# Attention and gated FFN on one core: the second product of the output projection earlier, and VectorE's multiplications of P @ v ahead of the joining step and the subtraction

## The chip, the core and the metric

The kernel runs on one core of a Trainium2 chip. The metric is the device time of one execution in microseconds (us); the median of several executions counts. Engines: TensorE (PE in the profile, its weight loads PEld), VectorE (DVE), ScalarE (ACT), GpSimd (POOL), and SyncE (SP), which issues the transfers here. Each engine has its own list of instructions.

## The reference

Input is 8 sequences of 256 tokens with 512 features, all float32. One attention layer and one FFN layer, each behind a layer norm and with a residual:

```
x = x + attention(layernorm(x))         # 32 query heads, 8 key/value heads, D = 128
x = x + ffn(layernorm(x))

attention: q, k, v = x @ w_qkv
           scores = q k^T / sqrt(128) - slope[head] * sqrt(distance), causal
           out = softmax(scores) @ v, then @ w_o
ffn:       dense = x @ weight.T + bias
           hits = softmax(x @ centroids.T / 0.1) > 0.01
           out  = dense where the row has a hit and the column's cluster has one, else 0
```

## The kernel before

**Units and slots.** The eight sequences form four pairs p of 512 tokens. For each pair and each key/value head kv there is a group g = 8 p + kv, and each group has two units, one for each sequence of the pair: u = 2 g + bb. A unit is the attention of four query heads over one sequence. The main loop (line 660) runs over the units; one turn of it is called a slot here, and `slot = u % 16` (line 663) says where in the pair it stands. Even slots have bb = 0, odd ones bb = 1. A slot takes about 22 us and holds three units at different stages:

- of unit u: the scores on TensorE (L376 and L382), scaled and biased by VectorE (L378, L384), and the maxima of the softmax;
- of unit u − 1: the subtraction of the maxima, two thirds by GpSimd (L428) and one third by VectorE (L431), the exponential by ScalarE (L754), and its sums;
- of unit u − 2: the product P @ v on TensorE (L452, L453; `attend`), VectorE's multiplication by the inverse sums (L456, two of them, one for each two heads, which write oT), and the output projection (`project_out`, whose matmuls are L474).

Keys lie on the partitions, so a maximum or sum over keys goes over partitions. `over_keys` does it in three VectorE steps: two reductions with a 32x32 transpose (L393 over the first 128 keys, L394 over the others) and the joining step (L396), which combines the two. `over_quadrants` (called from `rows` and `rows_max`) does the rest: TensorE transposes the small tile r (L403, tile tp_r), VectorE reduces it to a row, and SyncE writes the row to HBM and reads it back broadcast to all partitions (tile bc). The next slot's subtraction and multiplication use bc.

**Seven products.** All projections are done by a scheme with seven matrix products instead of eight (as Strassen's). Sums of the operand's blocks are named S1 to S4 for one side and T1 to T4 for the other; S3 is written over block A21. A step function takes the number of a product: steps 1, 6, 7, 4 go one after the other into one PSUM bank and are copied out by ScalarE after each; a copy must be done before the next of them starts. Step 2 goes into a bank of its own and VectorE adds it; steps 5 and 3 share a bank, and VectorE adds after each. The factors: step 1 takes A11 and B11, step 2 A12 and B21, step 5 S1 and T1, step 6 S2 and T2, step 7 S3 and T3, step 3 S4 and B22, step 4 A22 and T4. Three such projections run interleaved in a slot:

- `qq(i)`: the q projection of the next group (tiles ps_qa, ps_qb, ps_qc), spread over the even slot (1, 2, 6, 7) and the odd one (4, 5, 3);
- `e(i)`: in slots 0, 1, 8, 9 the v projection (ps_va, ps_vb, ps_vc), in slots 3, 7, 11, 15 the k projection (ps_ka, ...), in the others nothing;
- `w(i)`: the output projection of unit u − 2 (ps_oa, ps_ob, ps_oc). Its sums S1 to S4, tile o_s, are made by GpSimd out of oT (lines 112 to 118, called at line 783). A11 and A12 are parts of oT itself.

For the v projection the sums S3 and S4 of the weights are made by VectorE in slots 0 and 8 (line 746, tile wv and e_t). In slots 11 and 12 the normed tokens of the next pair are transposed (`x(i)`, tile tpx, copied out by ScalarE, one PSUM bank). Pairs 1 and 2 carry the FFN of the pair before in slots 3 to 6 (`f(part)`). `norm(part)` computes layer norms; its square root and the exponential need different tables of ScalarE, so a table load stands before the first exponential after a norm.

**Order.** There is no scheduler: `tc.manual_schedule()` keeps every engine's instructions in the order of the program text. That order is the list of calls at lines 798 to 820, one for even slots, one for odd ones, and others for the first and last slots. An instruction waits for its inputs and for its buffers, and everything behind it on its engine waits with it. `max_and_old` (line 740) issues the third scores, the maxima of unit u (L393, L394, L396), the subtraction L431 for unit u − 1, and in slots 0 and 8 S3 and S4. `exp_old` issues L754.

Of the kernel before, what the change touches and what calls it, by code (L numbers as in the profile page):

```python
# [17 lines left out]
ALU = mybir.AluOpType  # L18
AX = mybir.AxisListType
# [4 lines left out]
G = NH // NKV  # L24
# [29 lines left out]
def block_kernel(  # L54
# [12 lines left out]
    nc = tc.nc  # L67
# [21 lines left out]
    gp, ve = nc.gpsimd.tensor_tensor, nc.vector.tensor_tensor  # L89
# [17 lines left out]
    def a_sums(tt, a, which="S1 S2 S3 S4"):  # L107
        for s in which.split():
            if callable(a[s]):
                a[s] = a[s]()  # L110
            if s == "S1":
                tt(a["S1"], a["A21"], a["A22"], ALU.add)  # L112
            elif s == "S2":
                tt(a["S2"], a["S1"], a["A11"], sub)
            elif s == "S3":
                tt(a["S3"], a["A11"], a["A21"], sub)
            else:
                tt(a["S4"], a["A12"], a["S2"], sub)
# [64 lines left out]
    wv, wk, wq, wo = {}, {}, {}, {}  # L183
# [176 lines left out]
    K0, K1 = G * S, G * P  # L360
    J0, J1 = K0 // 32, K1 // 32
    s_sb, inv_sb, bc_sb = {}, {}, {}
# [24 lines left out]

    def over_keys(s, r, which, op):  # L390
        a, b = which * J0, 2 * J0 + which * J1
        first, second = r[:, a : a + J0], r[:, b : b + J1]
        nc.vector.tensor_reduce(first, s[:, :K0].rearrange("p (j q) -> p j q", q=32), AX.X, op, apply_transpose=True)  # L393
        nc.vector.tensor_reduce(second, s[:, K0:].rearrange("p (j q) -> p j q", q=32), AX.X, op, apply_transpose=True)  # L394
        late = first.rearrange("p (h i) -> p h i", h=G)[:, :, 4:8]
        nc.vector.tensor_tensor(late, late, second.rearrange("p (h i) -> p h i", h=G), op)  # L396

    def over_quadrants(u, r, has_max, has_sum):

# [24 lines left out]
    def subtract_max(u, i):  # L424
        s, mx = s_sb[u], bc_sb[u][:, 0]
        if i == 0:
            k0 = s[:, :K0].rearrange("p (h q) -> p h q", h=G)
            gp(k0, k0, mx, sub)  # L428
        else:
            k1 = s[:, K0:].rearrange("p (h q) -> p h q", h=G)  # L430
            ve(k1, k1, mx[:, :, P:], sub)  # L431
# [209 lines left out]
    k, q = project_k(0, 0), project_q(0)  # L641
# [18 lines left out]
    for u in range(NU + 2):  # L660
        g, bb = divmod(u, 2)
        p, kv = divmod(g, NKV)
        slot = u % SPP
        own, old, out_ = u < NU, 0 < u <= NU, u >= 2
        more_q, more_p = own and g + 1 < NG, own and p + 1 < NPAIR
        r = small.tile([P, 2 * (J0 + J1)], F32, tag="r", name="r", bufs=2) if own or old else None
# [13 lines left out]
        e, qq = nothing, nothing  # L680
        if own and u > 0 and slot in (0, 1, 8, 9):
            e = project_v(p, slot // 8, bb)
        elif own and slot in (3, 7, 11):
            e = project_k(p, (slot + 1) // 4)
        elif more_p and slot == 15:
            e = project_k(p + 1, 0)
        if more_q:
            if bb == 0:
                q = project_q(g + 1)
            qq = q  # L690
        ww = {}

        def w(*steps):
            for i in steps:
                if out_:
                    if i == 1:
                        ww[0] = project_out(u - 2)
                    ww[0](i)


        t_ffn = None
        if own and 3 <= slot < 7 and 0 < p < NPAIR - 1:
            t_ffn = (p - 1) * TPP + slot - 3
# [3 lines left out]
        def f(part):  # L707
            if t_ffn is not None:
                if part == 0:
                    ffn_transpose(t_ffn)  # L710
                elif part == 1:
                    ffn_second(t_ffn, w_ffn)
                elif part == 1.5:
                    ffn_first(t_ffn, w_ffn)
                    ffn_max(t_ffn)
                    ffn_exp(t_ffn)
                elif part == 2:
                    ffn_bias_add(t_ffn, y_late[:, t_ffn % TPP, :] if t_ffn >= first_late else None)
                else:
                    ffn_hits(t_ffn)  # L720
                    ffn_qsel(t_ffn)
                    ffn_end(t_ffn)
# [12 lines left out]
        def norm(part):  # L735
            nonlocal found
            if t_norm is not None:
                found = (lambda _: norm_stats(t_norm, t_norm + 1), norm_root, norm_scale, norm_write)[part](found)

        def max_and_old():  # L740
            scores(u, 2)
            over_keys(s_sb[u], r, 0, ALU.max)
            if u > 1:
                subtract_max(u - 1, 1)
            if u > 0 and slot in (0, 8):
                a_sums(ve, wv[p, slot // 8], "S3 S4")

        def more_sums():
            if more_p and slot == 14:
                sum_x(p + 1, "T3 T4")  # L750

        def exp_old():
            if u > 1:
                nc.scalar.activation(s_sb[u - 1], s_sb[u - 1], AF.Exp)  # L754

        def sum_old():
            if old:
                over_keys(s_sb[u - 1], r, 1, ALU.add)
# [3 lines left out]
        def rows_max():  # L762
            if alone:
                over_quadrants(u, r, True, False)

        def rows():
            if old:
                over_quadrants(u, r, own and not alone, True)

        def behind_rows():  # L770

            f(3)
            norm(2)
            if own and (slot == 7 or slot == 15 and more_p):
                sum_weights(ve, wv, (p, 1) if slot == 7 else (p + 1, 0), HH, "S1 S2")
            if more_p and slot == 13:
                sum_x(p + 1, "T1 T2")

        def av(i):
            if out_:  # L780
                attend(u - 2, i)
                if i == 1:
                    a_sums(gp, o_sb[u - 2][1])

        def x(i):
            if more_p and slot in (11, 12):
                norm_tile(p + 1, 2 * (slot - 11) + i)

        if u == 0:
            k(3), max_and_old()  # L790
            sum_weights(ve, wv, (0, 0), HH, "")
            e = project_v(0, 0, 0)
            q_first("5p"), e(1), e(2), q_first(5), q_first(3), rows_max()
            a_sums(ve, wv[0, 0])
            qq(1), e(6), qq(2), e(7), e(5), qq(6), e(4), e(3), qq(7)
            subtract_max(0, 0), subtract_max(0, 1)
            nc.scalar.activation(s_sb[0], s_sb[0], AF.Exp)
        elif bb == 0 and own:
            qq(1), e(1), max_and_old(), e(2), f(0), av(0), e(6), exp_old(), av(1), more_sums(), f(1), rows_max(), f(1.5), e(7), qq(2)
            if u == 4:  # L800
                onehot_of_columns(asg)
            f(2), norm(0), e(5), e(4), qq(6), e(3), x(0), w(1), x(1), sum_old(), w(5, 6), norm(1), qq(7), w(2)
            rows(), behind_rows(), w(7, 3), norm(3), w(4)
        elif u < NU - 1:
            e(1), qq(4), e(2), max_and_old(), f(0), e(6), av(0), exp_old(), e(7), av(1), f(1), f(1.5), e(5), qq(5)
            f(2), norm(0), e(4), e(3), x(0), w(1), x(1), sum_old(), w(5, 6), norm(1), qq(3), w(2)
            rows(), behind_rows()
            if u == NU - 3:
                found_late = norm_scale(norm_root(found_late))
            w(7, 3), norm(3), w(4)  # L810
        elif own:

            max_and_old(), f(0), av(0), exp_old(), av(1), rows_max(), f(1), f(1.5)
            f(2), w(1), sum_old(), w(5, 6), w(2)
            rows(), subtract_max(u, 0), subtract_max(u, 1)
            w(7)
            norm_write(found_late)
            nc.scalar.activation(s_sb[u], s_sb[u], AF.Exp)
            w(3), w(4)
            t_old = t_ffn  # L820
        elif bb == 0:
            sum_old(), av(0), f(0), av(1), f(1), rows()
            ffn_first(t_ffn, w_ffn), w(1, 5)
            ffn_max(t_ffn), ffn_exp(t_ffn)
            f(2), w(6)
            flush_adds()
            ffn_hits(t_old), ffn_qsel(t_old), ffn_end(t_old)
            w(2, 7)
            flush_adds()
            w(3, 4)  # L830
            found = norm_stats(last, last + 1)
            t_old = t_ffn
        else:
            av(0), f(0)
            found = norm_scale(norm_root(found))
            av(1), norm_write(found, tags=("y", "y")), f(1)
            ffn_hits(t_old), ffn_qsel(t_old), ffn_end(t_old)
            ffn_max(t_ffn), ffn_exp(t_ffn)
            w(1, 2, 5, 6, 3)
            found = norm_root(norm_stats(last + 2))  # L840
            w(7)
            ffn_transpose(last, "bc")
            ffn_transpose(last + 1, "snap", tp=p_long.tile([P, 512], F32, tag="aq", name="tpx_late"))
            norm_write(norm_scale(found))
            w(4)
            normalise(norm_stats(last + 3))
            ffn_first(t_ffn, w_ffn)
# [144 lines left out]
```

## Time and profile before

| what | value |
|---|---|
| median of 3 runs | 1426.2 us (1426.0 to 1427.32) |
| profiled execution, its time | 1425.68 us |
| profiled execution, its span | 1423.9 us |
| TensorE clock granted | 0.999 |
| busy: VectorE, GpSimd, ScalarE | 933.7, 878.9, 370.9 us |
| the chain that ended last: PE, DVE, issue, POOL | 91%, 6%, 1%, 1% |
| exponential L754 (128x1536) | 62 times, mean 1484 ns |
| GpSimd's subtraction L428 (128x1024) | 64 times, mean 2372 ns |
| joining step L396 (128x16) | 128 times, min 174, median 272, max 2101 ns |

The span runs from the first instruction to the last in one profiled execution; the execution's time has 1.8 us around it. In the lists of waits, a line gives the engine, the tile and line that waited, after the arrow who released it, then the total, the number and the longest of these waits in us. In a timeline, a line gives the start, the length, the engine, the line of the kernel, the operation, output and inputs with their shapes, and in brackets how long the engine had idled before and who ended that. A line "x4" merges four records; a float32 matmul leaves two records.

### The profile page before, as it was taken

Reading aid. Unit: us, or ns where it says so; the run is one execution under the profiler, and the core shown is the slowest. Engines: PE = TensorE matmul, PEld = TensorE weight load, DVE = VectorE, ACT = ScalarE, POOL = GpSimd, SP = SyncE. Lnnn points to the kernel's source line nnn. Section 1 sums busy time; section 2 is a strip of 40 time slices with the busy share of each in tenths; the row PEclk is TensorE's granted clock in tenths of the full one; section 3 lists DMA queues with packets and bytes.
Section 4 is the critical chain, followed back from the end, with each engine's and each line's share of the span. In section 5 each row is a group of like instructions: output and inputs, shape, how many; then the busy total and the mean of one; then the engine's idle time right before and its main releaser. Section 6 shows DMA issues by size and latency. Waiting matters only on the chain.

```text
span 1423.9 us, 16581 instructions
## 1 busy us (share of the span) xinstructions
PE 1402.3 (98%) x5867; PEld 1082.6 (76%) x5867; DVE 933.7 (66%) x1723; ACT 370.9 (26%) x649; POOL 878.9 (62%) x878
## 2 busy tenths in 40 slices
PE   9999999999999999999999999999999999999997
PEld 7777777767878777777777777777787778777674
DVE  5557666686566665668656667566766566556878
ACT  2222223411232222341223222243222122212332
POOL 5587857767465654668656466565756666476663
PEclk9999999999999999999999999999999999999999
DMA  5335343443242544423334435344314342333343
GB/s 188 119 106 175 123 125 132 144 148 128 96 167 75 178 141 157 157 81 142 126 113 143 132 120 178 126 156 149 133 60 148 130 168 88 148 102 125 133 163 118
DMA packets 87312, 190.20 MB, mean 134 GB/s; under 512 B 11616, under 2 KB 20064, under 8 KB 87232
## 3 DMA queue, kind: packets, MB, share of 16 engines
q1 hardware_dynamic: 86320, 187.59, 38.5%
q10 hardware_dynamic: 864, 1.44, 0.3%
q8 instruction: 47, 0.77, 0.2%
q14 instruction: 33, 0.27, 0.1%
q0 software_dynamic: 48, 0.13, 0.0%
HBM read 176.03 MB, written 13.11 MB: 133 GB/s over the span
## 4 chain that ended last, share of the span: by engine, by line
PE 91%; DVE 6%; issue 1%; POOL 1%; ACT 0%; DMA 0%; DVEq 0%; POOLq 0%; ACTq 0%
PE ps_oa L474 15%; PE ps_qa L145 14%; PE ps_oc L474 8%; PE sc L376 7%; PE ps_qc L145 7%; PE av L452 7%; PE ps_ka L145 4%; PE sc L382 4%; PE ps_va L145 4%; PE ps_ob L474 4%; PE av L453 3%; PE ps_qb L145 3%; PE ps_vc L145 2%; PE ps_kc L145 2%; PE ps_lg L520 2%; PE ps_f L520 1%
## 5 line engine op out<-in xcount | busy, mean ns | idle before, releaser
L428 POOL TENSOR_TENSOR s<-s,bc 128x1024 f32<-128x1024 f32 x64 | 151.8, 2372 | 157.3 <-DMA bc<-row_hbm 157.2
L506 POOL TENSOR_TENSOR x<-x,snap 128x256 f32<-128x256 f32 x189 | 136.0, 736 | 162.6 <-DVE x L494 92.8
L393 DVE TRANSPOSE_TENSOR_REDUCE r<-s 128x32 f32<-128x1024 f32 x128 | 157.9, 1234 | 5.5 <-ACT s L754 4.5
L112 POOL TENSOR_TENSOR o_s<-oT 128x256 f32<-128x256 f32 x64 | 47.7, 746 | 179.2 <-DVE oT L456 173.7
L161 ACT COPY qT<-ps_qa 128x512 f32<-128x512 f32 x128 | 74.8, 584 | 287.2 <-PE ps_qa L145 287.2
L489 ACT COPY snap<-ps_oa 128x256 f32<-128x256 f32 x189 | 70.4, 373 | 273.3 <-PE ps_oa L474 273.2
L474 PE MATMUL ps_oa<-wo,oT 128*128 128x256 f32 x512 | 133.1, 382 | 3.4 <-DVE oT L456 3.4
L754 ACT ACTIVATE s<-s 128x1536 f32<-128x1536 f32 x62 | 92.0, 1484 | 151.4 <-DVE s L431 140.6
L452 PE MATMUL av<-s,v 128*128 128x512 f32 x256 | 130.7, 592 | 0.0
L145 PE MATMUL ps_qa<-xT,wq 128*128 128x256 f32 x512 | 121.0, 379 | 0.0
L376 PE MATMUL sc<-qT,kT 128*128 128x512 f32 x256 | 120.4, 592 | 0.0
L145 PEld LDWEIGHTS ps_qa<-xT,wq 128*128 128x128 f32 x512 | 97.0, 190 | 26.2 <-issue 14.6
L378 DVE SCALAR_TENSOR_TENSOR s<-sc,alibi 128x512 f32<-128x512 f32 x128 | 88.0, 690 | 32.8 <-PE sc L376 32.0
L474 PEld LDWEIGHTS ps_oa<-wo,oT 128*128 128x128 f32 x512 | 90.7, 190 | 22.8 <-DVE oT L456 7.1
L384 DVE SCALAR_TENSOR_TENSOR s<-sc,alibi 128x512 f32<-128x512 f32 x64 | 44.3, 692 | 81.3 <-PE sc L382 81.3
L453 PEld LDWEIGHTS av<-s,v 128*128 128x128 f32 x256 | 48.6, 190 | 61.2 <-issue 61.2
L456 DVE TENSOR_TENSOR oT<-av,bc 128x512 f32<-128x512 f32 x128 | 83.9, 681 | 11.4 <-PE av L453 9.6
L394 DVE TRANSPOSE_TENSOR_REDUCE r<-s 128x16 f32<-128x512 f32 x128 | 85.6, 669 | 0.0
L453 PE MATMUL av<-s,v 128*128 128x256 f32 x256 | 76.1, 379 | 0.0
L396 DVE TENSOR_TENSOR r<-r 128x16 f32<-128x16 f32 x128 | 72.5, 566 | 4.4
L376 PEld LDWEIGHTS sc<-qT,kT 128*128 128x128 f32 x256 | 48.5, 190 | 34.0 <-issue 29.2
L494 DVE TENSOR_TENSOR x<-x,ps_ob 128x256 f32<-128x256 f32 x64 | 26.9, 421 | 71.6 <-PE ps_ob L474 71.5
(195 smaller groups left out, 2974.5 us busy)
## 6 DMA issues: line engine op xcount, KB each, us to landing
bc<-row_hbm SPq DMA_DIRECT2D x128, 512.0 KB, 4.9
wq<-in_w_qkv SPq DMA_DIRECT2D x32, 1024.0 KB, 7.8
wo<-in_w_o SPq DMA_DIRECT2D x32, 1024.0 KB, 7.9
alibi<-al_hbm SPq DMA_DIRECT2D x24, 512.0 KB, 8.5
wk<-in_w_qkv SPq DMA_DIRECT2D x16, 512.0 KB, 9.4
wv<-in_w_qkv SPq DMA_DIRECT2D x8, 1024.0 KB, 10.7
x<-in_x SPq DMA_DIRECT2D x16, 256.0 KB, 9.2
al_hbm<-alibi SPq DMA_DIRECT2D x8, 512.0 KB, 8.8
```

What stands on the lines that cost most here:

```text
L145: nc.tensor.matmul(bank[:, cols], lhsT=lhsT, rhs=rhs, start=first and j == 0, stop=j == len(mms) - 1, skip_group_check=True)
L376: nc.tensor.matmul(sc, lhsT=kT[:, t0 : t0 + P], rhs=qT[:, hh : hh + 2, t0 : t0 + S], start=True, stop=True)
L378: nc.vector.scalar_tensor_tensor(s[:, hh * S : (hh + 2) * S], sc, D ** -0.5, bias[:, hh : hh + 2, :].rearrange("p h q -> p (h q)"), ALU.mu ...
L393: nc.vector.tensor_reduce(first, s[:, :K0].rearrange("p (j q) -> p j q", q=32), AX.X, op, apply_transpose=True)
L394: nc.vector.tensor_reduce(second, s[:, K0:].rearrange("p (j q) -> p j q", q=32), AX.X, op, apply_transpose=True)
L428: gp(k0, k0, mx, sub)
L452: nc.tensor.matmul(av, lhsT=v[:, i0, vc], rhs=pT[:, hh * S : (hh + 2) * S], start=True, stop=False)
L453: nc.tensor.matmul(av3[:, :, P:S], lhsT=v[:, i0 + 1, vc], rhs=pT[:, K0 + hh * P : K0 + (hh + 2) * P].rearrange("p (h q) -> p h q", h=2), s ...
L456: ve(oT[:, e].rearrange("p k m q -> p k (m q)"), av3, inv[:, hh : hh + 2, :], ALU.mult)
L474: nc.tensor.matmul(bank[:, :HH], lhsT=x[:, e, :], rhs=y[:, e, :], start=first and e == 0, stop=e == 1, skip_group_check=True)
L506: gp(c, c, s, ALU.add)
L754: nc.scalar.activation(s_sb[u - 1], s_sb[u - 1], AF.Exp)
```

## The change

- `over_keys` gets a parameter that lets the two reductions and the joining step be issued separately.
- `max_and_old` now issues only the two reductions (from u = 2 on). The joining step, the subtraction L431 and the sums S3 and S4 go into a new function `late_max`, which is called behind `av(1)`. So on VectorE both multiplications L456 stand ahead of them. The exponential (`exp_old`) stays behind the subtraction.
- `w(2)` goes from behind `qq(7)` (even slots) or `qq(3)` (odd slots) to just behind `w(1)`, ahead of `w(5)` and `w(6)`.
- In odd slots `e(7)` goes from ahead of `av(1)` to behind it and `exp_old`; in even slots `e(7)` and `qq(2)` change places.
- In slots 4 and 12 without FFN work (u = 4, 12, 28, 44, 52, 60), `rows()` comes ahead of `qq(7)`.

The instructions of GpSimd, ScalarE and SyncE keep their order, and no instruction is added or taken away.

```diff
-    def over_keys(s, r, which, op):
+    def over_keys(s, r, which, op, parts="both late"):
         a, b = which * J0, 2 * J0 + which * J1
         first, second = r[:, a : a + J0], r[:, b : b + J1]
-        nc.vector.tensor_reduce(first, s[:, :K0].rearrange("p (j q) -> p j q", q=32), AX.X, op, apply_transpose=True)
-        nc.vector.tensor_reduce(second, s[:, K0:].rearrange("p (j q) -> p j q", q=32), AX.X, op, apply_transpose=True)
-        late = first.rearrange("p (h i) -> p h i", h=G)[:, :, 4:8]
-        nc.vector.tensor_tensor(late, late, second.rearrange("p (h i) -> p h i", h=G), op)
+        if "both" in parts:
+            for out_, keys in ((first, s[:, :K0]), (second, s[:, K0:])):
+                nc.vector.tensor_reduce(out_, keys.rearrange("p (j q) -> p j q", q=32), AX.X, op, apply_transpose=True)
+        if "late" in parts:
+            late = first.rearrange("p (h i) -> p h i", h=G)[:, :, 4:8]
+            nc.vector.tensor_tensor(late, late, second.rearrange("p (h i) -> p h i", h=G), op)
...
         def max_and_old():
             scores(u, 2)
-            over_keys(s_sb[u], r, 0, ALU.max)
-            if u > 1:
-                subtract_max(u - 1, 1)
-            if u > 0 and slot in (0, 8):
-                a_sums(ve, wv[p, slot // 8], "S3 S4")
+            over_keys(s_sb[u], r, 0, ALU.max, "both")
+            if not out_:
+                late_max(True)
+
+        def late_max(now=out_):
+
+            if own and now:
+                over_keys(s_sb[u], r, 0, ALU.max, "late")
+                if u > 1:
+                    subtract_max(u - 1, 1)
+                if u > 0 and slot in (0, 8):
+                    a_sums(ve, wv[p, slot // 8], "S3 S4")
...
         elif bb == 0 and own:
-            qq(1), e(1), max_and_old(), e(2), f(0), av(0), e(6), exp_old(), av(1), more_sums(), f(1), rows_max(), f(1.5), e(7), qq(2)
+            qq(1), e(1), max_and_old(), e(2), f(0), av(0), e(6), av(1), late_max(), exp_old(), more_sums(), f(1), rows_max(), f(1.5), qq(2), e(7)
...
-            f(2), norm(0), e(5), e(4), qq(6), e(3), x(0), w(1), x(1), sum_old(), w(5, 6), norm(1), qq(7), w(2)
-            rows(), behind_rows(), w(7, 3), norm(3), w(4)
+            f(2), norm(0), e(5), e(4), qq(6), e(3), x(0), w(1), x(1), sum_old(), w(2, 5, 6), norm(1)
+
+            if slot in (4, 12) and t_ffn is None:
+                rows(), qq(7)
+            else:
+                qq(7), rows()
+            behind_rows(), w(7, 3), norm(3), w(4)
         elif u < NU - 1:
-            e(1), qq(4), e(2), max_and_old(), f(0), e(6), av(0), exp_old(), e(7), av(1), f(1), f(1.5), e(5), qq(5)
-            f(2), norm(0), e(4), e(3), x(0), w(1), x(1), sum_old(), w(5, 6), norm(1), qq(3), w(2)
+            e(1), qq(4), e(2), max_and_old(), f(0), e(6), av(0), av(1), late_max(), exp_old(), e(7), f(1), f(1.5), e(5), qq(5)
+            f(2), norm(0), e(4), e(3), x(0), w(1), x(1), sum_old(), w(2, 5, 6), norm(1), qq(3)
             rows(), behind_rows()
...
-            max_and_old(), f(0), av(0), exp_old(), av(1), rows_max(), f(1), f(1.5)
+            max_and_old(), f(0), av(0), av(1), late_max(), exp_old(), rows_max(), f(1), f(1.5)
```

## The prediction

> **What bounds the kernel now.** I read the page's busy times first, then the waits of TensorE and of its weight loads, then the timeline of single slots.
>
> ```profile
> PE 1402.3 (98%) x5867; PEld 1082.6 (76%) x5867; DVE 933.7 (66%) x1723; ACT 370.9 (26%) x649; POOL 878.9 (62%) x878
> ```
> ```profile
> PEld ps_oa L474 <- DVE oT L456: 7.1, 13, 2.0
> PEld ps_oc L474 <- POOL o_s L112: 6.6, 10, 0.9
> PE ps_oa L474 <- DVE oT L456: 3.4, 3, 1.6
> PE ps_oc L474 <- POOL o_s L112: 2.5, 9, 0.5
> ```
>
> TensorE (PE) is busy for 1402 of 1423.9 us, so the order of the others matters only where PE waits. The waits that the change can touch are these: the output projection waiting for VectorE's product oT, and for GpSimd's sums o_s made of it. They come in few slots. The timeline of slot u = 13 shows one:
>
> ```profile
> 294.42 2.35 POOL L428 TENSOR_TENSOR s<-s,bc 128x1024 f32<-128x1024 f32 x1 [5.38 <-DMA bc<-row_hbm]
> 294.60 1.89 PE L145 MATMUL ps_qc<-xT_t,wq_s 128*128 128x256 f32 x8
> 294.69 2.10 DVE L396 TENSOR_TENSOR r<-r 128x16 f32<-128x16 f32 x1
> 296.72 0.68 DVE L431 TENSOR_TENSOR s<-s,bc 128x512 f32<-128x512 f32 x1
> 297.32 1.27 DVE L456 TENSOR_TENSOR oT<-av,bc 128x512 f32<-128x512 f32 x2
> 298.05 1.30 PE L474 MATMUL ps_oa<-wo,oT 128*128 128x256 f32 x4 [1.56 <-DVE oT L456]
> ```
>
> The tiny joining step L396 (elsewhere 0.18 us) lasts 2.10 us, until POOL's L428 ends at 296.77. L431 and both L456 queue behind it, and PE waits.
>
> PE's busy time hides part of such waits, so I use starts: in an undisturbed stretch, 8 matmul records of 256 columns take 1.73 us from start to start, 4 take 0.86. By that ruler PE lost in u = 13: 1.72 before w(1), 0.26 inside it, 0.44 at w(5), together 2.4.
>
> **What the skill says.** "SBUF — State Buffer", section "SBUF: two separate sides": VectorE and GpSimd share one port pair as an exclusive lock; a VectorE operation with two SBUF inputs against GpSimd blocks wholly, whoever comes first goes first. The trace agrees (L396 above). L456 reads PSUM and one SBUF tensor: beside L428 in u = 2 (70.43 to 71.72) it kept its 0.68 each. "PSUM — Partial Sum Buffer", section "Engine vs sequencer instructions": VectorE's and ScalarE's queues are strict FIFO, matmuls run in program order. The whole count below rests on that.
>
> **Part 1, oT before L396 and L431: what goes.** oT comes before the locked step. By the ruler, the waits at w(1), w(5), w(6) are: u2 0.4, u5 1.2, u13 2.4, u14 1.0, u29 0.8, u30 1.0, u45 0.5, u46 1.0, u50 0.3, u53 2.4, u61 0.5, together 11.5 us. All should go: oT moves up by 0.8 (0.18 + 0.69, overlapped) or by the whole lock time, and w(2) before w(5) gives the sums 0.86 us more. What is late next there is the transpose tp_r. In u = 13 r was ready 2.26 us before it; L428's row now leaves 1.7 earlier in slot 12, so I take no new wait. Gain: 11.5 (9.5 to 11.5).
>
> **Part 2, what L431 carries with it.** L431 now starts behind both L456, and the second needs the second P @ v. Behind L431 stand the exponential (L754), and on ScalarE's queue the evacuations behind that.
>
> *Odd slots with e, no table load* (17: u = 3, 7, 9, 15, 17, 23, 25, 31, 33, 39, 41, 47, 49, 51, 55, 57, 59). In u = 25, second P @ v ends at 563.83; e(7) now follows it, so 562.97. Second L456 starts 0.04 later, L396 0.60 later, L431 0.09 later (563.70), the exponential 0.78 after that: 564.48 instead of 562.91. e(7)'s copy ends 1.74 after that (564.30 + 0.35 − 562.91), at 566.22. e(4), at 566.26, needs it, and its weight load starts at 566.05. I price 0.12 (where PE waits for a copy at u = 1, the next start is late by another 0.10). Sum 2.0, bounds 0 and 5.
>
> *Slots 11 and 12, pairs 0 to 2.* There a table load stands before the exponential and waits for L431 as well:
>
> ```profile
> 254.66 1.28 ACT L754 ACT_TABLE_LOAD   x1 [2.09 <-DVE s L431]
> 255.96 1.49 ACT L754 ACTIVATE s<-s 128x1536 f32<-128x1536 f32 x1
> 257.35 0.35 ACT L161 COPY kT<-ps_ka 128x256 f32<-128x256 f32 x1
> 258.03 1.03 PE L145 MATMUL ps_ka<-xT_t,wk 128*128 128x256 f32 x4
> ```
> ```profile
> 279.08 0.59 ACT L161 COPY qT<-ps_qa 128x512 f32<-128x512 f32 x1
> 279.56 0.59 ACT L297 COPY xT<-tpx 128x512 f32<-128x512 f32 x1
> 280.21 0.66 PE L296 MATMUL tpx<-ident,xn 128*128 128x128 f32 x4
> ```
>
> ("ScalarE: Activation LUTs", section "What ACT_TABLE_LOAD costs", gives about 1283 ns for a load; here 1.28.) In u = 11 all is 1.57 later, the copy ends at 259.27, and e(4) wants it at 258.03: 1.30 with the 0.06 from copy to matmul, and 0.10: 1.4. In u = 12, L431 moves from 275.61 to 276.81; the copy of the first transposes ends at 281.34, not 280.15; the second group waits 1.2. Three times each: 4.2 + 3.6 = 7.8 (6 to 9).
>
> *Slots 0 and 8 (u = 8, 16, 24, 32, 40, 48, 56).* The sum S3 (L116) for e(7) moves with L431, while e(7) is put behind qq(2).
>
> ```profile
> 704.67 0.68 DVE L116 TENSOR_TENSOR wv<-wv 128x512 f32<-128x512 f32 x1
> 705.18 0.59 PE L453 MATMUL av<-s,v 128*128 128x256 f32 x2
> 705.61 1.03 PE L145 MATMUL ps_va<-wv,xT 128*128 128x256 f32 x4
> 707.56 0.72 POOL L112 TENSOR_TENSOR o_s<-oT 128x256 f32<-128x256 f32 x1 [4.28 <-DVE oT L456]
> ```
>
> P @ v ends at 705.77; second L456 705.81, L396 706.41, L431 706.50, L116 not before 707.10. But oT is then done at 706.50, so POOL's o_s asks for the port at 706.58, between the two. Such an alternation stands in u = 14: L129 starts at 317.56, POOL's L112 at 317.72, L131 ends at 319.37, 1.81 after L129's start. So L116 ends at 708.31 (707.79 without POOL) and e(7) starts 0.14 later (as at u = 56: 1219.21 to 1219.35), at 708.45; its place is 705.61 + 1.73 = 707.34. Loss 1.1 and 0.07: 1.2 (0.66 without POOL, 1.9 if POOL gets in twice). At u = 56, 1.0 of it is there already. Sum 6 x 1.2 + 0.2 = 7.4 (4 to 12).
>
> **Part 3, rows() before qq(7)** in u = 4, 12, 28, 44, 52, 60. tp_r is wanted 1.73 earlier. Slack was 3.2 to 3.8 except in u = 4: there the joining step ended at 118.81, tp_r started at 118.87. With VectorE some 0.4 earlier, PE waits 1.4 instead of 0.2: +1.2 (0.5 to 1.7). SP's order is unchanged; the row's two transfers only leave sooner.
>
> **Part 4, w(2) sooner.** Same matmuls; its add L494 stands behind the sums' reductions, and banks rotate with time to spare: 0.
>
> **Part 5, the tail.** In u = 63, rows_max follows P @ v on PE. tp_r at 1354.66 needed r at 1354.49; now the second L456 starts at 1354.86, L396 ends 1355.64: +1.1 (0.5 to 1.1), which the chain of waits (PE up to 1380) carries to the end.
>
> **Sum.** −11.5 + 2.0 + 7.8 + 7.4 + 1.2 + 1.1 = +8.0 us. The profiled execution took 1425.68 (span 1423.9 and 1.8 around it): 1433.7. The median shown is 0.5 above it: about 1434.
>
> **Rivals.**
>
> A: heavier. The exponential in the 17 odd slots is later still, since o_s on POOL takes the port between L396 and L431 (0.7 each, about 12 in all); part of it comes true: +6 to +10, so 1440 to 1444. Against it: L431 is issued 0.08 before POOL's request.
>
> B: faster. ScalarE's lateness does not reach PE: e(4) and the second transposes do not in fact stand on the late copies. That takes 9.8 away (2.0 + 7.8): −1.8; with L116 ahead of POOL (−3.1) it is −4.9, so 1421. It decides from about 8 us of lost stalls on. For it: in u = 25 the copy had 1.6 us of room, so my margin is a difference of two close numbers. Against: in u = 11 the room was 0.33 and in u = 12 it was 0.06.
>
> C: nothing moves: the waits that go and those that come are of one size, 1426. It needs the low ends of all bounds at once (−11.5 + 0 + 6 + 4 + 0.5 + 0.5 = −0.5).
>
> **How the numbers follow.** Forecast 0.60, A 0.20, B 0.12, C 0.08. A difference of 0.2% (2.9 us) is what a measurement here tells from none. Faster 0.11, same 0.08, slower 0.81. The range 1428 to 1442 leaves out B, most of C and the end of A. The forecast's own range is 1430 to 1439.
>
> **What would show it.** Right: waits of ps_oa and ps_oc for oT and o_s nearly gone; ps_va waiting for wv (L116) seven times, about 1.2 each; ps_ka and tpx waiting for ScalarE's copies in slots 11 and 12 of pairs 0 to 2; tp_r waiting in u = 4 and 63. Wrong: no wait of ps_va for wv, or e(4) on time in u = 11. A new wait in slots 5, 13 or 14 for tp_r would mean that the gain was mis-sized.

## The result, and the profile after

| kernel | median us | runs | profiled execution, its span |
|---|---|---|---|
| before | 1426.6 (1426.0 to 1428.06) | 5 | 1423.9 |
| changed | 1437.38 (1437.13 to 1438.46) | 5 | 1435.4 |

The ratio is 1.0076, 95% interval 1.0064 to 1.0087: the change costs 0.8%. TensorE does the same work in the same busy time. This is the line of busy times on the page of the changed kernel:

```profile
PE 1401.4 (98%) x5867; PEld 1087.7 (76%) x5867; DVE 903.5 (63%) x1723; ACT 368.9 (26%) x649; POOL 909.7 (63%) x878
```

So the 11.5 us of span are waits. The next lines are TensorE's longest waits in the changed kernel (released by whom, then total, number, longest):

```profile
PE ps_va L145 <- DVE wv L116: 6.7, 7, 1.0
PE tp_r L405 <- DVE r L398: 5.6, 7, 1.8
PE ps_ka L145 <- ACT kT L161: 3.4, 3, 1.1
PE tpx L296 <- ACT xT L297: 2.6, 3, 0.9
```

The lines of ps_oa for oT and of ps_oc for o_s, which led the list before, are gone. Four others lead it instead. (In the changed kernel's code the line numbers are higher: L396 is L398, L428 is L430, L431 is L433, L456 is L458, L754 is L763.) The timeline of u = 32 in the changed kernel shows how the first of them comes about:

```profile
710.89 0.17 DVE L398 TENSOR_TENSOR r<-r 128x16 f32<-128x16 f32 x1
...
710.97 0.69 DVE L433 TENSOR_TENSOR s<-s,bc 128x512 f32<-128x512 f32 x1
711.05 1.19 POOL L112 TENSOR_TENSOR o_s<-oT 128x256 f32<-128x256 f32 x1 [2.94 <-DVE r L398]
711.58 1.22 DVE L116 TENSOR_TENSOR wv<-wv 128x512 f32<-128x512 f32 x1
...
712.94 1.10 PE L145 MATMUL ps_va<-wv,xT 128*128 128x256 f32 x4 [0.96 <-DVE wv L116]
```

S3 (L116) stands behind both multiplications, the joining step and the subtraction. On top of that it lasts 1.22 us where it took 0.68 before, because GpSimd's first sum o_s gets the port between L433 and L116. TensorE waits 0.96 us for it. GpSimd pays too; this is the group of that sum on the page of the changed kernel (the mean was 746 ns before):

```profile
L112 POOL TENSOR_TENSOR o_s<-oT 128x256 f32<-128x256 f32 x64 | 74.5, 1165 | 139.0 <-DVE r L398 132.1
```

Nothing on TensorE waits for that: its list has no line of ps_oc for o_s, here or in the run below that puts w(2) back behind w(5).

A cleaner account than the waits is the length of each slot, from the first score matmul of a unit to that of the next. Of the 61 slots before u = 61, those that are not named in this table differ by less than 0.03 us between the two kernels. (The prediction had 0.5 of its 11.5 in u = 61; it stands in the tail's row here.)

| slots | predicted us | measured us, changed minus before |
|---|---|---|
| u = 2, 5, 13, 14, 29, 30, 45, 46, 50, 53 (waits for oT and o_s) | −11.0 | −10.9 |
| 17 odd slots with e | +2.0 | +2.0 (17 x 0.12) |
| u = 11, 27, 43 | +4.2 | +4.2 (3 x 1.40) |
| u = 12, 28, 44 | +3.6 | +3.0 (3 x 1.00) |
| slots 0 and 8 | +7.4 | +7.4 (6 x 1.20 and 0.20) |
| u = 4 | +1.2 | +1.7 |
| from u = 61 to the end | +0.6 (−0.5 + 1.1) | +4.0 |
| before u = 2 | 0 | +0.1 |
| sum | +8.0 | +11.5 |

### The profile page after: what moved, and what is told of

Same layout as the page of the kernel before. It is cut to its first block, busy times and chain, and to the rows that moved or that the text cites. A ratio compares the mean times of both kernels' runs of the same rounds, so it can differ in the third digit from the quotient of the medians.

```text
span 1435.4 us, 16583 instructions
## 1 busy us (share of the span) xinstructions
PE 1401.4 (98%) x5867; PEld 1087.7 (76%) x5867; DVE 903.5 (63%) x1723; ACT 368.9 (26%) x649; POOL 909.7 (63%) x878
## 4 chain that ended last, share of the span: by engine, by line
PE 87%; DVE 8%; ACT 2%; issue 1%; POOL 1%; DMA 1%; SPq 0%; DVEq 0%; ACTq 0%; POOLq 0%
PE ps_qa L145 14%; PE ps_oa L476 14%; PE sc L376 7%; PE ps_oc L476 7%; PE ps_qc L145 7%; PE av L454 7%; PE ps_va L145 4%; PE sc L382 4%; PE ps_ka L145 4%; PE ps_ob L476 4%; PE av L455 3%; PE ps_qb L145 2%; PE ps_vc L145 2%; PE ps_kc L145 2%; PE ps_lg L522 2%; PE ps_f L522 1%
## 5 line engine op out<-in xcount | busy, mean ns | idle before, releaser
L395 DVE TRANSPOSE_TENSOR_REDUCE r<-s 128x32 f32<-128x1024 f32 (+1 forms) x256 | 234.0, 952 | 17.9 <-ACT s L763 17.1
L430 POOL TENSOR_TENSOR s<-s,bc 128x1024 f32<-128x1024 f32 x64 | 150.8, 2356 | 134.7 <-DMA bc<-row_hbm 134.6
L112 POOL TENSOR_TENSOR o_s<-oT 128x256 f32<-128x256 f32 x64 | 74.5, 1165 | 139.0 <-DVE r L398 132.1
L763 ACT ACTIVATE s<-s 128x1536 f32<-128x1536 f32 x62 | 92.0, 1484 | 208.9 <-DVE s L433 208.8
L376 PE MATMUL sc<-qT,kT 128*128 128x512 f32 x256 | 120.4, 593 | 0.0
L458 DVE TENSOR_TENSOR oT<-av,bc 128x512 f32<-128x512 f32 x128 | 83.7, 673 | 24.4 <-PE av L455 16.3
L502 DVE TENSOR_TENSOR x<-x,ps_oc 128x256 f32<-128x256 f32 x128 | 53.3, 417 | 38.3 <-PE ps_oc L476 37.4
L476 PE MATMUL ps_oa<-wo_t,o_s 128*128 128x256 f32 x256 | 65.9, 380 | 0.9 <-DVE x L489 0.9
L382 PE MATMUL sc<-qT,kT 128*128 128x512 f32 x128 | 65.9, 597 | 0.5 <-DVE s L378 0.5
## 6 DMA issues: line engine op xcount, KB each, us to landing
wv<-in_w_qkv SPq DMA_DIRECT2D x8, 1024.0 KB, 11.5
```

What stands on the lines that cost most here:

```text
L376: nc.tensor.matmul(sc, lhsT=kT[:, t0 : t0 + P], rhs=qT[:, hh : hh + 2, t0 : t0 + S], start=True, stop=True)
L382: nc.tensor.matmul(sc, lhsT=kT[:, t0 + P : t0 + S], rhs=qT[:, :, t0 + P : t0 + S], start=True, stop=True)
L395: nc.vector.tensor_reduce(out_, keys.rearrange("p (j q) -> p j q", q=32), AX.X, op, apply_transpose=True)
L458: ve(oT[:, e].rearrange("p k m q -> p k (m q)"), av3, inv[:, hh : hh + 2, :], ALU.mult)
L476: nc.tensor.matmul(bank[:, :HH], lhsT=x[:, e, :], rhs=y[:, e, :], start=first and e == 0, stop=e == 1, skip_group_check=True)
```

## The experiments

**The second product alone.** The kernel before with w(2) behind w(1) and nothing else:

```diff
-            ... w(1), x(1), sum_old(), w(5, 6), norm(1), qq(7), w(2)
+            ... w(1), x(1), sum_old(), w(2, 5, 6), norm(1), qq(7)
```

(and the same with qq(3) in odd slots).

> The kernel before with one part of the change alone: w(2) goes from behind qq(7) or qq(3) to behind w(1). My theory (the waits at single slots add up): the waits at w(5) and w(6) for o_s go, 6.3 us by the starts in the trace of before, and the waits at w(1) for oT (5.2 us) stay; nothing is made late. So about 6.3 us faster than before, 1420.3. Rival 1 (GpSimd and VectorE collide on the shared port more, and that is what costs): w(2) moves no operation of the two against each other, so no change, or the gain is unclear. Rival 2 (the earlier w(2) itself is the harm, through its bank or its add on VectorE): slower than before by up to 11 us.

Measured: 1416.87 us (1416.02 to 1420.63), ratio to the kernel before 0.9937 (0.9921 to 0.9952). That is more than expected: without any change of VectorE's order, the ten slots with waits for oT and o_s are 12.0 us shorter, where the whole change takes away 10.9. (New waits in u = 4, 12, 24, 28, 44 and 56 give 2.0 back. And 1.3 of the 12.0 is another wait: the third scores of u = 14, 30 and 46 come 0.4 us late in the kernel before and in the changed one. VectorE's sum L125 ahead of them lasts 1.6 to 1.8 us there, and in u = 14 a GpSimd sum has started just before it; here VectorE starts first, and L125 takes 0.71.) So the waits of w(1) for oT in u = 5, 13 and 53 went too, though w(1) has not moved. The timeline of u = 13 in this kernel says how:

```profile
291.14 2.37 POOL L428 TENSOR_TENSOR s<-s,bc 128x1024 f32<-128x1024 f32 x1 [3.13 <-DMA bc<-row_hbm]
```
```profile
293.67 0.18 DVE L396 TENSOR_TENSOR r<-r 128x16 f32<-128x16 f32 x1
293.77 0.69 DVE L431 TENSOR_TENSOR s<-s,bc 128x512 f32<-128x512 f32 x1
294.37 1.28 DVE L456 TENSOR_TENSOR oT<-av,bc 128x512 f32<-128x512 f32 x2
```

In the kernel before, L428 ran from 294.42 to 296.77 and held L396 for 2.10 us. Here it ends at 293.51, before L396 begins: its input bc arrived earlier. The two timelines of SyncE show that the write of the row in u = 12 took 3.62 us until the read could be issued in the kernel before (286.53 to 290.15), and 1.77 here (285.29 to 287.06). The transfers tell the reason. First the kernel before, 286.4 to 290.2 us, in 40 slices (GB/s is what they moved), then this one, 285.2 to 287.1:

```profile
GB/s 0 0 0 0 0 0 0 0 0 0 0 0 0 225 27 1 0 0 0 0 0 0 0 0 0 0 3 3 0 0 0 0 0 0 0 0 0 0 0 0
...
q8 instruction: 1, 0.02, 2.2%
q1 hardware_dynamic: 80, 0.01, 1.6%
```
```profile
GB/s 0 0 0 0 0 0 0 0 0 0 0 0 0 0 0 0 0 0 0 0 0 0 0 0 0 49 46 49 27 3 0 0 0 345 0 0 0 0 0 0
...
q8 instruction: 1, 0.02, 3.1%
q1 hardware_dynamic: 80, 0.01, 3.0%
```

The row is 80 small packets. In each window there is one fetch of instructions of 16 KB besides (0.02 MB on the line). In the kernel before the fetch starts together with the row, and the row's last five packets (the two 3s) come 1.3 us after its first ones, when the fetch has ended. Here the fetch starts behind the row's last packet, and the write is not late. The row is early by 0.22 us against the end of its slot: with w(2) moved, its add L494 no longer stands on VectorE between tp_r and the row's reduction.

**The row earlier, by another edit.** The kernel before with rows() ahead of w(2), which leaves w(2) and VectorE's order as they are:

```diff
-            ... norm(1), qq(7), w(2)
-            rows(), behind_rows(), ...
+            ... norm(1), qq(7)
+            rows(), w(2), behind_rows(), ...
```

> The kernel before with one edit: rows() ahead of w(2) instead of behind it, in even and odd slots; w(2) stays behind qq(7) or qq(3), and VectorE's order in max_and_old is untouched. The transposes tp_r and the write of the row then come 0.86 us sooner. Theory: the large waits for oT in the kernel before (u = 5, 13 and 53; 1.2, 2.4 and 2.4 us) came from a row write that fell together with a fetch of instructions and took 2.4 to 3.6 us instead of 1.7 to 1.8, so that GpSimd's subtraction came late and held the joining step; a write at another moment misses the fetch, and these 6.0 us go, without any change of VectorE's order; the waits of w(5) for o_s (u = 14, 30, 46) stay in part. About 1420, between 1417 and 1422; against it, tp_r in u = 4 may wait about 0.9. Rival, that the waits for oT need w(2) behind w(1) or the multiplications ahead of the joining step: 1425 to 1428.

Measured: 1420.86 us (1420.65 to 1421.88), ratio 0.9968 (0.9956 to 0.9981), as expected. u = 13 is 1.9 shorter, u = 53 1.9, u = 5 0.7, u = 4 0.8 longer; u = 14, 30 and 46 keep their waits for o_s within 0.1. So the largest waits that the change was to remove hung on the moment of a row write, and most of the others on the place of w(2) (u = 50 and a third of u = 29 went here too). In none of the other kernels traced is the write of u = 12 or u = 52 late: it was bad luck of the kernel before.

**The rest of the change without the second product.** The changed kernel with w(2) back behind qq(7) or qq(3); rows() stays ahead of qq(7) where the change put it, with w(2) just ahead of rows() there:

```diff
-            ... sum_old(), w(2, 5, 6), norm(1), qq(3)
+            ... sum_old(), w(5, 6), norm(1), qq(3), w(2)
```

(and the same in even slots).

> The changed kernel with w(2) back behind qq(7) or qq(3); all else as changed. By the trace of the changed kernel, the first sum S1 ends at least 0.09 us before the start of what would then be w(5), so with the multiplications ahead w(2) is not needed: 0 to 1 us slower than the changed kernel (weight loads start 0.2 ahead and could be late in seven slots), 1437.4 to 1438.4. If instead w(2) carries the part of the gain at w(5) and w(6), 6 us slower: 1443.5. If w(2) is the harm (rival 2): faster, towards 1426.

Measured: 1440.33 us (1439.38 to 1444.54), ratio 1.0102 (1.0085 to 1.0119): 3.0 above the changed kernel, 2 more than the upper expectation. The list of TensorE's waits for this kernel has a new line:

```profile
PE ps_oa L476 <- ACT snap L491: 2.1, 8, 0.6
```

w(6) uses the bank of w(1) and waits for ScalarE's copy of it. That copy is behind the exponential, which the change made late, and only w(5) is left between. With w(2) there too, it is covered. The timeline of u = 13 in this kernel:

```profile
302.54 1.48 ACT L763 ACTIVATE s<-s 128x1536 f32<-128x1536 f32 x1 [4.66 <-DVE s L433]
...
303.93 0.35 ACT L491 COPY snap<-ps_oa 128x256 f32<-128x256 f32 x1
...
304.42 1.10 PE L476 MATMUL ps_oa<-wo_t,o_s 128*128 128x256 f32 x4 [0.21 <-ACT snap L491]
```

Four kernels thus make a square: before 1426.7, w(2) alone 1416.9, the rest alone 1440.3, both 1437.4. The second product is worth 9.9 alone, but 3.0 beside the rest; the rest costs 13.6 alone and 20.5 beside the second product. The rest is VectorE's reordering together with the moves of e(7), qq(2) and rows(); the next runs take it apart.

**The old order in slots 11 and 12** of pairs 0 to 2; the edit adds a switch to the changed kernel (as in two later runs):

```diff
+        early = not out_ or more_p and slot in (11, 12)
...
-            if not out_:
+            if early:
                 late_max(True)
```

> The changed kernel, but in slots 11 and 12 of pairs 0 to 2, the ones with a table load, the joining step and the subtraction stay ahead of both multiplications. My theory: the waits of ps_ka for ScalarE's copy in slot 11 (3 times 1.39 us in the trace of the changed kernel) and of the transposes in slot 12 (3 times 1.09) go, 7.4 us: 1430.0. Rival 1 (the shared port in all slots): 6 of 62 slots are undone, about 1 us, near 1436.4.

Measured: 1430.66 us (1430.48 to 1434.36), ratio 1.0035 (1.0024 to 1.0046). The slots lose 4.2 and 2.7 us, where 4.2 and 3.3 were expected.

**The old order in slots 0 and 8**, the same switch with `slot in (0, 8)`:

> The changed kernel, but in slots 0 and 8 the joining step, the subtraction and the sums S3 and S4 stay ahead of both multiplications, as before. My theory: e(7) finds S3 ready in all seven slots, 7 times 1.2 us go: 8.4 us faster than the changed kernel, 1429.0; no wait of ps_va for wv is left. Rival 1 (the shared port in all slots): 7 of 62 slots are undone, so about a ninth of the 11 us comes back, near 1436.

Measured: 1436.74 us (1434.95 to 1439.34), ratio 1.0071 (1.0053 to 1.0088): nothing won, against the expectation. The seven slots are 1.0 us shorter in sum, not 7.4. The timeline of u = 8 in this kernel:

```profile
190.79 0.18 DVE L398 TENSOR_TENSOR r<-r 128x16 f32<-128x16 f32 x1
190.88 0.68 DVE L433 TENSOR_TENSOR s<-s,bc 128x512 f32<-128x512 f32 x1
...
191.49 0.69 DVE L116 TENSOR_TENSOR wv<-wv 128x512 f32<-128x512 f32 x1
...
192.09 0.68 DVE L118 TENSOR_TENSOR e_t<-wv,e_t 128x512 f32<-128x512 f32 x1
192.69 0.41 DVE L165 TENSOR_TENSOR v<-v,ps_vb 128x256 f32<-128x256 f32 x1
...
193.16 1.99 PE L145 MATMUL ps_qb<-xT,wq 128*128 128x256 f32 x8 [0.56 <-DVE v L165]
```

S3 is in time, but qq(2), which the change put ahead of e(7), is not. It waits for the add of e(2) (L165), which now has four instructions ahead of it again. The wait has only changed its owner. So both edits of the slot were undone:

```diff
-            ... more_sums(), f(1), rows_max(), f(1.5), qq(2), e(7)
+            ... more_sums(), f(1), rows_max(), f(1.5)
+            if early:
+                e(7), qq(2)
+            else:
+                qq(2), e(7)
```

> The changed kernel, but in slots 0 and 8 both edits of the slot are undone: the joining step, the subtraction, S3 and S4 stay ahead of the multiplications, and e(7) stays ahead of qq(2). In e2_old_0_8 the first alone was undone; ps_va no longer waited for wv, but ps_qb waited for VectorE's add of v (7 times, 0.73 to 1.76), since qq(2) came 0.86 sooner and its bank waits for that add behind S3 and S4. Theory: with both undone neither wait is left, except about 1 us in u = 56: 7.4 below the changed kernel's 1437.4, about 1430. Rival, that the time in slots 0 and 8 comes from something else in them: 1435 to 1437.

Measured: 1431.56 us (1430.36 to 1433.74), ratio 1.0043 (1.003 to 1.0057), near the expected 1430. The seven slots lose 7.1 us. The profiled execution (span 1432.0) also has 3.7 us in u = 28, where the read of bc with the inverse sums landed 7.9 us after its issue (5.4 in the changed kernel); why, is open.

**Only S3 and S4 ahead** of the multiplications, with qq(2) left ahead of e(7):

```diff
             over_keys(s_sb[u], r, 0, ALU.max, "both")
+            if u > 0 and slot in (0, 8):
+                a_sums(ve, wv[p, slot // 8], "S3 S4")
...
-                if u > 0 and slot in (0, 8):
-                    a_sums(ve, wv[p, slot // 8], "S3 S4")
```

> The changed kernel, but in slots 0 and 8 the sums S3 and S4 of wv stand ahead of the multiplications, right behind the two reductions; the joining step and the subtraction stay behind the multiplications, and qq(2) stays ahead of e(7). Theory: of what was moved behind the second P @ v, only S3 costs anything in these slots, and the add that frees the bank of ps_qb is not late as it was in e2_old_0_8, since it has only S3 and S4 ahead of it, without the joining step and the subtraction (0.8 less): 7 to 8 us below the changed kernel's 1437.4, about 1430. Rival one, ps_qb waits as in e2_old_0_8: 1435 to 1437. Rival two, the late exponential costs in these slots too: above 1432.

Measured: 1432.24 us (1430.62 to 1435.16), ratio 1.0053 (1.0038 to 1.0069); the slots lose 5.6 us: 0.94 in six of them, nothing in u = 24, where ps_qb waited 0.85. So S3 is most of the cost there. In the six, 0.25 us each stays: e(4) waits for the copy of e(7) behind the late exponential, which is the second rival at a small size.

**e(7) ahead of av(1) in odd slots:**

```diff
-            ... e(6), av(0), av(1), late_max(), exp_old(), e(7), f(1), ...
+            ... e(6), av(0), e(7), av(1), late_max(), exp_old(), f(1), ...
```

> The changed kernel, but in odd slots e(7) stands ahead of av(1), as in the kernel before; the multiplications stay ahead of the joining step and the subtraction. The second P @ v then ends 0.86 us later, and with it everything that VectorE and ScalarE have behind it. Theory: in the 17 odd slots with the v or k projection, e(4) stands on the copy of e(7) with no room left (0.10 of wait each in the changed kernel), so the wait there grows by 0.86; the same in slot 11 of pairs 0 to 2: 17 x 0.86 + 3 x 0.86 = 17 us above the changed kernel's 1437.4, about 1454. Rival, that the odd slots have room and the 0.10 is only the width of a release: 1437 to 1440.

Measured: 1431.9 us (1431.32 to 1432.37), ratio 1.0052 (1.0036 to 1.0069): 5.5 below the changed kernel where 17 above was expected. Both theories fell, since I had overlooked one of the instructions that the edit moves: ScalarE's copy of e(7) is issued with e(7), and so went ahead of the exponential. The timeline of u = 11 in this kernel:

```profile
256.10 0.37 ACT L161 COPY kT<-ps_ka 128x256 f32<-128x256 f32 x1 [1.78 <-PE ps_ka L145]
...
258.84 1.28 ACT L763 ACT_TABLE_LOAD   x1 [2.37 <-DVE s L433]
...
259.78 1.03 PE L145 MATMUL ps_ka<-xT_t,wk 128*128 128x256 f32 x4
```

The subtraction and the exponential are later still, as expected, but e(4) needs only the copy, done 3.3 us before. All 17 odd slots lose their 0.12 and u = 11, 27 and 43 lose 1.33 each: 6.0 in sum. This settles what those slots stood on: not VectorE's late work itself, but the copy of e(7) behind the late exponential.

**The tail and u = 4:** the switch with `u >= NU - 3`, and `and u != 4` for rows() ahead of qq(7).

> The changed kernel, but with the old order (joining step and subtraction ahead of the multiplications) in u = 61 to 63, and rows() behind qq(7) in u = 4. Theory: the changed kernel's trace has 4.3 us more of waits from u = 61 on than the one before, nearly all of tp_r for r, and 1.8 us in u = 4; both go: about 1431.3. Rival, that the tail is bound by FFN work, GpSimd or transfers, so that time won at tp_r is lost behind it: about 1435.6, only the 1.8 of u = 4.

Measured: 1433.84 us (1432.23 to 1436.18), ratio 1.0067 (1.0052 to 1.0082). The median lies between the theory and the rival. The trace decides for the theory: u = 4 is 1.7 shorter, and from u = 61 to the end it is 3.3 shorter (108.8 us after 112.1; before the change 108.2). Of TensorE's waits for r this is left:

```profile
PE tp_r L405 <- DVE r L398: 1.1, 2, 0.7
```

**The version that the runs point to:** the kernel before with w(2) behind w(1), S3 and S4 ahead of the joining step, and rows() ahead of qq(7) in slot 12 of pairs 0 to 2.

```diff
-            over_keys(s_sb[u], r, 0, ALU.max)
-            if u > 1:
-                subtract_max(u - 1, 1)
+            over_keys(s_sb[u], r, 0, ALU.max, "both")
             if u > 0 and slot in (0, 8):
                 a_sums(ve, wv[p, slot // 8], "S3 S4")
+            over_keys(s_sb[u], r, 0, ALU.max, "late")
+            if u > 1:
+                subtract_max(u - 1, 1)
...
+            if more_p and slot == 12:
+                rows(), qq(7)
+            else:
+                qq(7), rows()
```

> The kernel before with w(2) behind w(1) (as in e1), with S3 and S4 of slots 0 and 8 ahead of the joining step and the subtraction instead of behind them, and with rows() ahead of qq(7) in slot 12 of pairs 0 to 2. The multiplications stay behind the joining step. What e1 still shows of waits: ps_va for wv in u = 24 and 56 (0.6 and 1.2), tpx in u = 28 and 44 (0.6 and 0.3). Theory: these go, 2.5 us below e1's 1416.9, so about 1414.5. Rival, that the joining step and the subtraction, 1.3 us later in slots 0 and 8, bring ScalarE's copies late there as they did in slots 11 and 12: 1418 to 1424.

Measured: 1416.01 us (1415.24 to 1416.67), ratio 0.9933 (0.9921 to 0.9945). It beats both kernels, but cannot be told from w(2) alone (0.9937). Its main loop is 1.0 us shorter: ps_va no longer waits, but ps_qb takes over part of that (0.3 in u = 24, 0.6 in u = 56).

## Why the prediction was right, and where its sum was off

The likeliest case came true by its own steps. Forecast 1434.0, measured 1437.4: right in sign and in what the change delays, 3.4 low; the cause of the largest waits that go was read only in part.

- **Waits for oT and o_s.** Predicted −11.0 in the ten slots (u = 61 aside), measured −10.9. The size is right, the cause only in part: the largest waits, in u = 13 and 53, were laid to VectorE's order, and a late row write stood behind them. The prediction noted that the row leaves 1.7 us earlier in slot 12 and did not count it as a second way to the same gain; how much the earlier multiplications do there by themselves, no run separates.
- **Odd slots with e, slot 11, slots 0 and 8.** 2.0, 4.2 and 7.4, all as predicted, to 0.1 us. The decisive margins held, narrow as they were (0.04 us in u = 25: the copy at 566.22, e(4) at 566.26). The alternation on the port held too: L116 was to last 1.21 us and lasted 1.22. The run with e(7) ahead shows the copy as the cause in odd slots; the runs with S3 ahead and with both edits undone show S3 as the main cause in slots 0 and 8. The 0.8 us or more for ps_qb in the run that undid one edit is no second cause in the changed kernel, where the add of e(2) stands ahead of the joining step; it comes of undoing half of a pair.
- **Slot 12.** 1.0 instead of 1.2 each.
- **u = 4.** Mis-sized: 1.7 instead of 1.2. I took r as 0.4 us earlier there, but it came at 118.76 in place of 118.81: the reductions end 0.2 earlier, and the joining step then lasts 0.33 in place of 0.17.
- **The tail** is the term that failed, put at +0.6 (1.1 in u = 63, less the 0.5 of u = 61) and measured at 4.0. The wait of tp_r in u = 63 came (0.96, below). But the same order also stands in u = 61 and 62. In u = 61 the 0.5 went, and a new wait of tp_r of 0.4 takes its place. In u = 62 the multiplications wait 1.61 us for bc, and the joining step now waits with them; tp_r is late there by 0.6 for the maxima and again by 0.7 for the sums behind the later exponential, and u = 63 repeats it with 1.1 and 0.8. The tail's run gave 3.3 of the 4.0 back. The last 0.6 is a race for the port behind u = 63, which that run loses too.

First u = 62 in the changed kernel, then the tp_r of u = 63:

```profile
1347.23 1.29 DVE L458 TENSOR_TENSOR oT<-av,bc 128x512 f32<-128x512 f32 x2 [1.61 <-DMA bc<-row_hbm]
1348.44 0.17 DVE L398 TENSOR_TENSOR r<-r 128x16 f32<-128x16 f32 x1
...
1348.75 0.27 PE L405 MATMUL tp_r<-ident,r 128*32 128x128 f32 x1 [0.43 <-DVE r L398]
```

```profile
1363.03 1.35 DVE L458 TENSOR_TENSOR oT<-av,bc 128x512 f32<-128x512 f32 x2
...
1364.29 0.17 DVE L398 TENSOR_TENSOR r<-r 128x16 f32<-128x16 f32 x1
...
1364.61 0.27 PE L405 MATMUL tp_r<-ident,r 128*32 128x128 f32 x1 [0.96 <-DVE r L398]
```

And the race, before and after. VectorE's small sum and GpSimd's sum start 0.01 us apart in both kernels; before, VectorE's was over in 0.23 us, after the change it takes 0.80, and an add that w(6) waits for is late by that much:

```profile
1384.12 0.82 POOL L114 TENSOR_TENSOR o_s<-o_s,oT 128x256 f32<-128x256 f32 x1
1384.13 0.23 DVE L573 TENSOR_TENSOR hits_any<-hits_any,e 128x64 f32<-128x64 f32 x1
```
```profile
1394.99 0.72 POOL L114 TENSOR_TENSOR o_s<-o_s,oT 128x256 f32<-128x256 f32 x1
1395.00 0.80 DVE L575 TENSOR_TENSOR hits_any<-hits_any,e 128x64 f32<-128x64 f32 x1
```

- **w(2) sooner was put at 0** beside the 11.5, to which it was to add only 0.86 us of room for the sums. The sum does not show the fault, since the waits can be taken away only once, but the reading was incomplete: w(2) alone takes nearly all of them, and the rest of the change was a second way to the same gain, at a price of 20.5. Of the 12.0 us that w(2) saves in the ten slots, about 4.5 come from the better moment of the row write (so much goes in u = 5, 13 and 53 with rows() first alone). That part is luck: nobody had planned it.
- **The rivals.** A (1440 to 1444) named the right place, o_s taking the port, but not the right victim: it delayed S3 (inside the 1.2), not the exponential in odd slots, where the wait was 0.12. B fell with u = 11. C would have needed all the low ends.

## What to carry to other kernels

Before you pay for a reordering, try each of its edits alone: two edits that remove the same waits do not add up, and here the cheap one was worth 9.9 us, nearly half of it by luck of the row's moment, and the pair cost 10.7. When an instruction is moved, follow everything that is issued with it on every engine; the copies behind a late exponential, not the moved instructions themselves, set most of the odd slots, and I missed such a copy once myself. A slot-by-slot difference of lengths tells such edits apart to 0.01 us (slots that no edit touched agree to 0.002), where medians do it to 2 or 3; but each trace is one execution, and a chance event such as the 3.7 us in u = 28 is in it too.

## What the hardware showed that was not expected

A small transfer can be hit by a fetch of instructions. The 8 KB row write usually took 1.7 to 1.8 us from its issue to the issue of the read that waits for it. In 11 of the 67 row writes of the kernel before it took 2.4 to 4.0 us, and in each of these the trace has a packet of 16 KB on the queue named "instruction" that started between 0.2 us before the issue and 1.8 us after it and took 0.9 to 1.4 us. In ten of the 11, five of the row's 80 packets start only as the fetch ends (0.015 us before its end), up to 1.7 us behind the row's first packet. No write without such a fetch took over 1.81 us; two with a fetch that started about 1.5 us after the issue, when the row's last packet had gone, were not late. Which writes are hit differs from kernel to kernel, as the order moves rows and fetches against each other: 4 in the changed one, and with rows() first none that stands still so long (3 took 2.0 to 2.2 us). Through the row, GpSimd's subtraction and its lock of the port, two such hits (u = 12 and 52) brought most of two stalls of TensorE of 2.4 us (1.9 of each went with rows() first). That the five packets wait on the same DMA engine as the fetch is my reading, which their share, 5 of 80 with 16 engines, fits; the records don't name the engine.

VectorE and GpSimd take turns on their operations with two SBUF inputs, where each queue has the next one ready: L433, o_s, L116, o_s. The Trainium skill ("SBUF — State Buffer", section "SBUF: two separate sides") calls the shared ports an exclusive lock for whoever comes first. The trace agrees and adds the price of a sequence: L116 lasts 1.22 us in place of 0.68, and GpSimd's first sum 1165 ns in the mean in place of 746.
